# A rest group's expands in four row quadrants, rank rows copied as soon as their table is done, down's rank rows in one visit, and down's weight sums in two pieces

## The chip, the cores and the metric

The kernel runs on one core of a Trainium2 chip. The metric is the device time of one execution in microseconds (us). Everything is computed in float32. In the profile PE is TensorE (matmuls) and PEld its weight loads, DVE is VectorE, ACT is ScalarE, POOL is GpSimd, and SP is the queue that issues most DMA transfers.

## The reference

Eight sequences of 256 tokens with 1024 features pass four layers, each added to its input. Every layer picks low-rank adapters (rank 16) by an index per sequence:

```python
x = x + L0(x)   # x W^T + b, plus 2 * (x A) B            (A, B of 32 adapters)
x = x + L1(x)   # gate/up/down with 2752 hidden features, adapters on all three
x = x + L2(x)   # (x B^T) A^T only                        (64 adapters)
x = x + L3(x)   # (x B^T) A^T only                        (8 adapters)

# inside L1, SCALE = 0.5
gate = x @ W_gate.T + 0.5 * (x @ A_gate.T) @ B_gate.T
up   = x @ W_up.T   + 0.5 * (x @ A_up.T)   @ B_up.T
act  = silu(gate) * up
down = act @ W_down.T + 0.5 * (act @ A_down.T) @ B_down.T
```

The change touches L1 alone.

## The kernel before

**Blocks and banks.** The 2048 tokens are two blocks of 1024 (`blk`), and each block is two banks of 512 tokens (`n`), two sequences to a bank. Layer 0 is done for both blocks first, then gate/up, down, and the layers 2 and 3 of block 0, then those of block 1. Activations are kept transposed: features lie on the 128 partitions and tokens along the free dimension. A PSUM bank holds 128 x 512 values.

**Strassen-like products.** The large products are done as seven products of half-size blocks in place of eight, once outside and once more inside. `Quads.step` (L464) issues one outer product as seven inner blocks of matmuls (`block`, L473 to L482, all of them line L476), with adds on DVE and copies on ACT between them (`first` L504, `more` L509, `whole` L517). The last inner block of a product is put into `pending` and issued in the middle of the next product (`flush`). The order of the outer products is `ORDER = (1, 2, 3, 5, 6, 7, 4)`. The weights' sums that this needs are made on POOL: `inner_sums` and `outer` for gate/up, `Down.sum_weights` (L610) for down.

**Groups of gate/up.** The 2752 hidden features are cut into five groups of 512 (`job`, L998) and a rest of 192 (`rest`, L1099). In a block the rest comes first. A group gives four results: E (gate, bank 0), Z (up, bank 0), Y (up, bank 1) and X (gate, bank 1), which are done after the second, fifth, sixth and seventh outer product. In the code `table` 0 is gate and 1 is up. As a result is done, its `done(n, table, c)` is called.

**The rest group.** Its weights have 256 columns per table: gate has 192 features and then, in `wrem`, the up table's last 64; the up table has 128 features and then the adapters' shrink weights A_gate and A_up. So the second half of the up result holds the rank rows x A: 64 partitions of ranks, 16 for each sequence and table. When both tables of a bank are done, `done` in `rest` (L1117) puts this into the list `beside`:

- `spread(j)` for j = 0 and 1 (L1128): four ACT copies of 32 partitions of rank rows into the four quadrants of a PSUM bank, then a DVE product with a mask into `t`, the tile that the profile calls trep (L1135);
- `lora` (L1140): four matmuls of K = 32 with N = 512 from trep and the gathered B rows, all of them line L989 in `expand_gu`, into the three banks `lo` that the profile calls plr: gate's first 128 features from row quadrant 0, up's first 128 from row quadrant 0, and the last 64 of each, both from row quadrant 1, into the lower and upper half of the third bank;
- `gates` (sigmoids on ACT, L1149) and the adds and products on DVE (L1164 to L1169) that make the hidden rest `hr`, and then `hidden`, which puts the shrink for down (`shrink_hidden`, line L261) on PE.

In a full group `lora` (L1019 and before, tile pl) puts the four 128-feature chunks in the four quadrants, since the gathered table has 512 columns there: quadrant r holds chunk r. For the rest the host pads 192 features to 512, so that quadrants 2 and 3 hold zeros. trep holds the same rank rows in all four quadrants.

**What sets the order of the work.** Each outer product is a `Unit` with eight slots, `at(0)` to `at(7)`. In a slot the unit calls the loads and sums that are due there, and then takes items off the front of `beside` until their costs reach the unit's share (L1507 to L1513):

```python
spent = 0
while beside and spent < u.share:
    cost, f = beside.popleft()
    f()
    spent += cost
```

An item of cost 9 that does nothing therefore fills one slot. The framework's scheduler then places each engine's instructions in one fixed order, which needn't be the order of these calls, and adds the semaphore waits. Engines run their instructions in that order. SBUF tiles of 8 KB per partition come from one pool of 22 (`big`), PSUM banks for small work from a pool of four (`ps_l`), so an allocation can make an instruction wait for an earlier tile's last reader.

**Down.** `down_projection` (L1192) does the 2048 features of the first four groups by `Down`, seven outer products of two tables, and the remaining 704 features by `job` (L1286). For each of the seven products, `sum_weights` makes four sums of 128 x 1024 on POOL (L614 to L617). The rank rows of down, `td`, were added up over the groups; `rank_rows` (L1245) brings them under the rest's 64 features in `hr`: for each bank one matmul of M = 32 with a picking matrix (L1250, tile prr) into 32 partitions of one PSUM bank, and one DVE operation from there into `hr` (L1251).

Of the kernel before, what the change touches and what calls it, by code (L numbers as in the profile page):

```python
# [11 lines left out]
ALU = mybir.AluOpType  # L12

P = 128
# [11 lines left out]
NN = TB // 512  # L26
F = 2752
FC = 21
FR = F - FC * P
# [3 lines left out]
REST = len(GROUPS) - 1  # L33
# [21 lines left out]
def kernel(  # L55
# [48 lines left out]
    nc = tc.nc  # L104
# [14 lines left out]
    def big(name):  # L119
        return upool.tile([P, BIG], F32, tag="u", name=name)  # L120

    def bank(pool, name):
        return pool.tile([P, 512], F32, tag=pool.name, name=name)
# [5 lines left out]
    start = big("start")  # L129
# [29 lines left out]
    mask = const.tile([P, 512], F32, tag="mask", name="mask")  # L159
# [17 lines left out]
    for r in range(4):  # L177
        rows = slice(32 * r, 32 * r + 32)
# [5 lines left out]
    for r in range(4):  # L184
        rows = slice(32 * r, 32 * r + 32)
# [5 lines left out]
    for r in range(4):  # L191
        rows = slice(32 * r, 32 * r + 32)
        nc.vector.tensor_copy(off_23[rows], sel_v[rows, 2 + r % 2, :, r // 2])
    nc.vector.tensor_scalar(off_23, off_23, float(R), rank_f, op0=ALU.mult, op1=ALU.add)
    for r in (1, 3):
        rows = slice(32 * r, 32 * r + 32)
# [20 lines left out]
    pick = const.tile([P, 32], F32, tag="pick", name="pick")  # L217
# [20 lines left out]
    def gather_a(table, layer, blk, name, pool=apool, tag="a", width=NC * R):  # L238
        t = pool.tile([P, BB * width], F32, tag=tag, name=name)
        t = t[:, : BB * table.shape[1]].rearrange("p (b w) -> p b w", b=BB)  # L240
        for q in range(BB):
            b = blk * BB + q
            gather(t[:, q, :], table, off_a[:, layer, b : b + 1])
        return t
# [40 lines left out]
    def copy(dst, src, scale=1.0):  # L285
        nc.scalar.activation(dst, src, AF.Identity, scale=scale)  # L286
# [4 lines left out]
    beside = deque()  # L291
# [264 lines left out]
    class Down(Quads):  # L556
# [53 lines left out]
        def sum_weights(self, s):  # L610
            w = self.w[s]
            a11, a21, a12, a22 = w[0][:, 0], w[0][:, 1], w[2][:, 0], self.both[s][:, 1]
            s2, s4, s3 = w[1][:, 0], w[1][:, 1], w[2][:, 1]
            nc.gpsimd.tensor_sub(s3, a11, a21)  # L614
            nc.gpsimd.tensor_add(a21, a21, a22)
            nc.gpsimd.tensor_sub(s2, a21, a11)
            nc.gpsimd.tensor_sub(s4, a12, s2)  # L617

        def sum_tokens(self, s):
            h, both = self.h[s], self.both[s]  # L620
# [334 lines left out]
    def gate_up(blk):  # L955
        st = sts[blk]
# [16 lines left out]
        def shrink_hidden(g, *halves):  # L973

            a, chunks = st["ad", g]
            pss = []
            for n, h in halves:
                pss.append(bank(ps_l, f"pd_{blk}_{g}_{n}"))
                for r in range(len(h)):
                    shrink_into(pss[-1], r, a, chunks, r, n, h[r], True, True)  # L980
            for (n, h), ps in zip(halves, pss):
                rows, td = slice(0, 32 * len(h)), st["td"][n]
                if g == REST:
                    nc.vector.memset(td, 0.0)
                nc.vector.tensor_add(td[rows], td[rows], ps[rows])

        def expand_gu(table, n, g, r, ps, cols=slice(0, P), outs=slice(0, P)):
            rows = slice(32 * r, 32 * r + 32)
            nc.tensor.matmul(  # L989
                ps[outs],  # L990
                st["bgu", g][rows, table, n, cols],
                st["t"][rows, table, n, :],
                start=True,
                stop=True,
                skip_group_check=True,
            )
# [102 lines left out]
        def rest():  # L1099

            held = {}

            def raw(key, t):
                kh, table = int(key[1]) - 1, int(key[2]) - 1
                if table == 0:
                    nc.sync.dma_start(out=t, in_=wrem[kh, 0])
                    return
                nc.sync.dma_start(out=t[:, :512], in_=wrem[kh, 1, :, :512])

                w = t[:, 512:].rearrange("p (c m) -> p c m", m=P)  # L1110
                for j in range(2):
                    a = st["agu"][j].rearrange("p b (r c) -> p c (b r)", c=NC)
                    nc.scalar.copy(
                        w[:, :, j * BB * R : (j + 1) * BB * R], a[:, kh * HC : (kh + 1) * HC, :]
                    )

            def done(n, table, c):  # L1117
                c = c.rearrange("p q i j t -> p (q i) (j t)")
                held[n, table] = c
                if (n, 1 - table) not in held:  # L1120
                    return
                g, u = held[n, 0], held[n, 1]
                if "t" not in st:
                    st["t"] = big(f"trep_{blk}").rearrange("p (g n t) -> p g n t", g=2, n=NN)
                    st["hr"] = big(f"hr_{blk}").rearrange("p (c n t) -> p c n t", c=2, n=NN)
                t, hr = st["t"], st["hr"]
                lo = []

                def spread(j):

                    src = slice(64 * j + 32 * n, 64 * j + 32 * n + 32)
                    ps = bank(ps_l, f"pt_{blk}_{n}_{j}")
                    for r in range(4):
                        copy(ps[32 * r : 32 * r + 32], u[src, 1, :], 0.5)
                    nc.vector.tensor_mul(t[:, j, n, :], ps, mask)  # L1135

                for j in range(2):
                    beside.append((0.69, lambda j=j: spread(j)))

                def lora():  # L1140
                    for j in range(3):
                        lo.append(bank(ps_l, f"plr_{blk}_{n}_{j}"))
                    expand_gu(0, n, REST, 0, lo[0])
                    expand_gu(1, n, REST, 0, lo[1])
                    for j in range(2):
                        half = slice(FR * j, FR * j + FR)
                        expand_gu(j, n, REST, 1, lo[2], slice(0, FR), half)

                def gates():  # L1149
                    nc.scalar.activation(lo[0], g[:, 0], AF.Sigmoid)  # L1150
                    nc.scalar.activation(lo[2][:FR], g[:FR, 1], AF.Sigmoid)

                    copy(u[:FR, 1], g[FR:, 1])

                left = slice(0, FR)

                def hidden():
                    nc.vector.memset(hr[FR:, 1, n], 0.0)
                    held["hr", n] = [hr[:, 0, n], hr[:, 1, n]]
                    if ("hr", 1 - n) in held:  # L1160
                        shrink_hidden(REST, *((n, held["hr", n]) for n in range(NN)))

                def multiply(to, x, y):
                    beside.append((0.69, lambda: nc.vector.tensor_mul(to(), x(), y())))  # L1164

                beside.append((0, lora))
                beside.append((0.69, lambda: nc.vector.tensor_add(g[:, 0], g[:, 0], lo[0])))
                beside.append((0.69, lambda: nc.vector.tensor_add(u[:, 0], u[:, 0], lo[1])))
                beside.append((0.69, lambda: nc.vector.tensor_add(g[:, 1], g[:, 1], lo[2])))  # L1169
                beside.append((0, gates))  # L1170
                for a, b, c in ((g[:, 0], 0, slice(0, P)), (g[left, 1], 2, left)):
                    multiply(lambda b=b, c=c: lo[b][c], lambda a=a: a, lambda b=b, c=c: lo[b][c])
                multiply(lambda: hr[:, 0, n], lambda: u[:, 0], lambda: lo[0])
                multiply(lambda: hr[left, 1, n], lambda: u[left, 1], lambda: lo[2][left])
                beside.append((1.2, hidden))

            q = Quads(blk, f"1_{blk}_r", 1, raw, done, SHARE_REST)

            def shrink_tables():
                st["agu"] = [  # L1180
                    gather_a(t, 1, blk, f"agu_{blk}_{j}") for j, t in enumerate((ag, au))
                ]

            q.units[0].ahead.insert(0, (3, 0, shrink_tables))
            q.units[0].before(2, 0, lambda: tables(REST))
# [6 lines left out]
    def down_projection(blk):  # L1192
        st = sts[blk]
# [51 lines left out]
        def rank_rows():  # L1245

            ps = bank(ps_l, f"prr_{blk}")
            for n in range(NN):
                rows = slice(64 + 32 * n, 96 + 32 * n)
                nc.tensor.matmul(ps[rows], pick, st["td"][n], start=True, stop=True)  # L1250
                nc.vector.scalar_tensor_tensor(  # L1251
                    st["hr"][rows, 1, n], ps[rows], 0.5, mask[rows], op0=ALU.mult, op1=ALU.mult
                )

        def load_w(o, g):
# [219 lines left out]
        for o in range(HC):  # L1475
            u = Unit(f"2_{blk}_{o}", lambda at, o=o: job(o, at), 1.2)
# [170 lines left out]
```

## Time and profile before

| what | value |
| --- | --- |
| median of 3 runs | 1804.67 us (1803.13 to 1806.73) |
| profiled execution, own time | 1805.19 us |
| its span, first to last instruction | 1803.4 us |
| mean granted TensorE clock | 0.998 |
| PE busy | 1790.4 us (99%) |
| DVE busy | 1051.5 us (58%) |
| POOL busy | 984.1 us (55%) |
| ACT busy | 298.6 us (17%) |
| DMA, mean over the span | 224 GB/s |

The profile is of one execution. A matmul of float32 stands in it as two records, and so does each weight load. Lengths of PE's records overlap, since matmuls are pipelined: the time that a piece of PE's work takes is read from its start to the start of the next piece. In the rows of the timeline, what stands in brackets is the idle time of the engine before the row and what ended it. "issue" means that the engine waited for nothing that the profile shows.

The chain of work that ended last is PE for 93% of the span. Its largest lines are the gate/up products (pa L476 26%, pc L476 13%, pb L476 6%), down's products (pa_d L476 11%, pc_d L476 5%, pb_d L476 3%) and L375 (pa 10%, pc 5%, pb 2%). The rest's products (pa_r L476) are 2% and the full groups' expands (pl L989) 2%.

### The profile page before, as it was taken

The numbers are of one execution on the slowest core, as the hardware profiler recorded it, in microseconds if no ns is written. First come the engines' busy times: TensorE is split into PE (matmuls) and PEld (weight loads), VectorE is DVE, ScalarE is ACT, GpSimd is POOL, SyncE is SP. The second block draws the span as 40 slices with busy tenths as digits, with TensorE's granted clock in tenths as the row PEclk, the third lists the DMA queues.
The fourth block names the chain that finished last, engine by engine and source line by source line (L and its number), as shares of the span: only waits on it lengthen the run. The fifth ranks groups of instructions, "written<-read, shape, count | busy, mean of one in ns | idle before, by whom it ended". The sixth has DMA issues, their size and how long they took to land.

```text
span 1803.4 us, 20672 instructions
## 1 busy us (share of the span) xinstructions
PE 1790.4 (99%) x7664; PEld 1312.2 (73%) x7664; DVE 1051.5 (58%) x1675; ACT 298.6 (17%) x536; POOL 984.1 (55%) x742
## 2 busy tenths in 40 slices
PE   9999999999999999999999999999999999999998
PEld 4444477888787878788854678787888887888743
DVE  5584255666666666748842464757575758554623
ACT  0121023020202121224210031121212121221000
POOL 6202579685868686344530567676767564443301
PEclk9999999999999999999999999999999999999999
DMA  6476895867676755778831865575848475745302
GB/s 233 172 281 250 273 396 184 304 225 287 215 294 208 298 187 217 260 272 311 316 135 67 307 264 192 176 292 171 296 165 290 166 256 184 255 165 180 110 0 94
DMA packets 119094, 403.38 MB, mean 224 GB/s; under 512 B 11858, under 2 KB 42706, under 8 KB 109522
## 3 DMA queue, kind: packets, MB, share of 16 engines
q1 hardware_dynamic: 108752, 382.24, 58.4%
q0 software_dynamic: 6080, 12.99, 2.3%
q10 hardware_dynamic: 4162, 6.82, 1.2%
q8 instruction: 62, 1.02, 0.2%
q14 instruction: 38, 0.31, 0.0%
HBM read 317.59 MB, written 84.41 MB: 223 GB/s over the span
## 4 chain that ended last, share of the span: by engine, by line
PE 93%; DVE 3%; issue 2%; DMA 1%; POOL 0%; ACT 0%; DVEq 0%; POOLq 0%; ACTq 0%; SPq 0%
PE pa L476 26%; PE pc L476 13%; PE pa_d L476 11%; PE pa L375 10%; PE pb L476 6%; PE pc_d L476 5%; PE pc L375 5%; PE pb_d L476 3%; PE pb L375 2%; PE pl L989 2%; PE pa_r L476 2%; PE pp L875 2%; PE pd L261 1%; PE pc_r L476 1%; DMA w_B<-in_wgu_dram 1%
## 5 line engine op out<-in xcount | busy, mean ns | idle before, releaser
L476 PE MATMUL pa<-tk,sw 128*128 128x256 f32 x1120 | 268.9, 383 | 1.7 <-DVE c_X L507 1.7
L476 PE MATMUL pc<-tk,sw 128*128 128x256 f32 x1120 | 264.9, 379 | 0.3 <-POOL sw L447 0.3
L476 PEld LDWEIGHTS pa<-tk,sw 128*128 128x128 f32 x1120 | 209.0, 190 | 59.9 <-issue 10.6
L476 PEld LDWEIGHTS pc<-tk,sw 128*128 128x128 f32 x1120 | 212.5, 190 | 31.2 <-issue 1.8
L476 PE MATMUL pa<-tk,w_B 128*128 128x256 f32 x960 | 227.8, 380 | 0.0
L476 PEld LDWEIGHTS pa<-tk,w_B 128*128 128x128 f32 x960 | 181.6, 190 | 32.5 <-issue 6.5
L446 POOL TENSOR_TENSOR sw<-w_B 128x512 f32<-128x512 f32 x60 | 76.5, 1275 | 170.8 <-PE pa L476 151.3
L614 POOL TENSOR_TENSOR dx_d<-dw_d 128x1024 f32<-128x1024 f32 x14 | 33.0, 2356 | 164.7 <-PE pa L476 44.3
L476 PE MATMUL pb<-tk,w_B 128*128 128x256 f32 x480 | 113.4, 379 | 0.0
L476 PE MATMUL pa_d<-dh_d,dw_d 128*128 128x256 f32 x448 | 102.2, 379 | 0.0
L476 PE MATMUL pc_d<-dh_d,dw_d 128*128 128x256 f32 x448 | 101.7, 379 | 0.0
L476 PEld LDWEIGHTS pb<-tk,w_B 128*128 128x128 f32 x480 | 91.2, 190 | 12.4
L507 DVE TENSOR_TENSOR c_X<-c_X,pa 128x512 f32<-128x512 f32 x90 | 61.5, 683 | 64.9 <-PE pa L476 64.9
L437 POOL TENSOR_TENSOR w_B<-w_B,w_B 128x1024 f32<-128x1024 f32 x40 | 93.4, 2356 | 2.4 <-PE pa L476 2.4
L476 PEld LDWEIGHTS pa_d<-dh_d,dw_d 128*128 128x128 f32 x448 | 85.0, 190 | 12.4 <-issue 0.8
L476 PEld LDWEIGHTS pc_d<-dh_d,dw_d 128*128 128x128 f32 x448 | 85.0, 190 | 12.4 <-issue 0.8
L448 POOL TENSOR_TENSOR sw<-w_B 128x512 f32<-128x512 f32 x60 | 87.8, 1463 | 0.0
L449 POOL TENSOR_TENSOR sw<-w_B,sw 128x512 f32<-128x512 f32 x60 | 80.6, 1343 | 3.9
L447 POOL TENSOR_TENSOR sw<-sw,w_B 128x512 f32<-128x512 f32 x60 | 76.9, 1282 | 0.0
L286 ACT ACTIVATE c_X<-pa 128x512 f32<-128x512 f32 x30 | 17.7, 591 | 341.1 <-PE pa L476 341.1
L231 POOL DMA_INDIRECT ad<-in_ad_dram,off_a x48 | 46.1, 961 | 31.3 <-PE pd L261 20.9
L375 PE MATMUL pa<-ht,wd 128*128 128x512 f32 x128 | 60.2, 600 | 0.0
(380 smaller groups left out, 3118.1 us busy)
## 6 DMA issues: line engine op xcount, KB each, us to landing
tk<-toks SPq DMA_DIRECT2D x140, 896.0 KB, 6.6
w_B<-in_wgu_dram SPq DMA_DIRECT2D x40, 1024.0 KB, 5.0
tk_r<-toks SPq DMA_DIRECT2D x28, 896.0 KB, 11.0
hk<-c_Z SPq DMA_DIRECT2D x32, 512.0 KB, 4.1
dh_d<-hk SPq DMA_DIRECT2D x14, 1024.0 KB, 8.4
hk<-c_Y SPq DMA_DIRECT2D x24, 512.0 KB, 4.1
x1d<-x SPq DMA_DIRECT2D x8, 1024.0 KB, 6.4
wo<-in_wd_dram SPq DMA_DIRECT2D x8, 1024.0 KB, 7.0
```

The lines of the kernel that those rows point to most:

```text
L231: nc.gpsimd.indirect_dma_start(out=t, out_offset=None, in_=table, in_offset=bass.IndirectOffsetOnAxis(ap=off, axis=0),)
L375: nc.tensor.matmul(ps, v[j], m[j], start=start and k == 0, stop=k == len(moving) - 1, skip_group_check=True,)
L437: f(self.raw[out][:, c], self.raw[a][:, c], self.raw[b][:, c])
L446: nc.gpsimd.tensor_add(s1, m21, m22)
L447: nc.gpsimd.tensor_sub(s2, s1, m11)
L448: nc.gpsimd.tensor_sub(s3, m11, m21)
L449: nc.gpsimd.tensor_sub(s4, m12, s2)
L476: nc.tensor.matmul(ps[:, q, :], w(j, q, kk), tok(j, kk), start=start and q == 0 and kk == 0, stop=kk == self.deep - 1, skip_group_check=True,)
L507: nc.vector.tensor_add(view(out, r, k), view(old, r, k), ps)
L614: nc.gpsimd.tensor_sub(s3, a11, a21)
L875: nc.tensor.matmul(pss[j, n], st["w", o][:, i, j // HC], x[c][n], start=i == 0, stop=i == NC - 1,)
L989: nc.tensor.matmul(ps[outs], st["bgu", g][rows, table, n, cols], st["t"][rows, table, n, :], start=True, stop=True, skip_group_check=True,)
```

## The change

There are four edits.

1. The rest's four expands take the row quadrants 0, 2, 1 and 3 in place of 0, 0, 1 and 1. For this the host repeats the padded 256 columns of B twice in place of padding to 512.
2. The rest's rank rows are copied as soon as the up table of a bank is done. For bank 0, where the gate table is done before, six empty items of cost 9 follow the copies, so that `lora` is called six slots later. For bank 1, where the up table is done first, the copies are put into `beside` one outer product earlier than before. The tiles trep and hr are allocated when the first result is done.
3. `rank_rows` issues both matmuls and then both DVE operations, in place of one after the other.
4. `sum_weights` makes each of the four sums in two pieces of 128 x 512. In the built program the two pieces of one sum stand next to each other on POOL.

```diff
@@ sum_weights
-            nc.gpsimd.tensor_sub(s3, a11, a21)
-            nc.gpsimd.tensor_add(a21, a21, a22)
-            nc.gpsimd.tensor_sub(s2, a21, a11)
-            nc.gpsimd.tensor_sub(s4, a12, s2)
+            for k in range(2):
+                c = slice(k * 512, k * 512 + 512)
+                nc.gpsimd.tensor_sub(s3[:, c], a11[:, c], a21[:, c])
+                nc.gpsimd.tensor_add(a21[:, c], a21[:, c], a22[:, c])
+                nc.gpsimd.tensor_sub(s2[:, c], a21[:, c], a11[:, c])
+                nc.gpsimd.tensor_sub(s4[:, c], a12[:, c], s2[:, c])
@@ rest: done
                 held[n, table] = c
-                if (n, 1 - table) not in held:
-                    return
-                g, u = held[n, 0], held[n, 1]
                 if "t" not in st:
                     st["t"] = big(f"trep_{blk}").rearrange("p (g n t) -> p g n t", g=2, n=NN)
                     st["hr"] = big(f"hr_{blk}").rearrange("p (c n t) -> p c n t", c=2, n=NN)
                 t, hr = st["t"], st["hr"]
                 lo = []
+                ranks, both = c, (n, 1 - table) in held
...
                     for r in range(4):
-                        copy(ps[32 * r : 32 * r + 32], u[src, 1, :], 0.5)
+                        copy(ps[32 * r : 32 * r + 32], ranks[src, 1, :], 0.5)
                     nc.vector.tensor_mul(t[:, j, n, :], ps, mask)
 
-                for j in range(2):
-                    beside.append((0.69, lambda j=j: spread(j)))
+                if table == 1:
+                    for j in range(2):
+                        beside.append((0.69, lambda j=j: spread(j)))
+                    if both:
+                        for _ in range(6):
+                            beside.append((9, lambda: None))
+                if not both:
+                    return
+                g, u = held[n, 0], held[n, 1]
 
                 def lora():
                     for j in range(3):
                         lo.append(bank(ps_l, f"plr_{blk}_{n}_{j}"))
-                    expand_gu(0, n, REST, 0, lo[0])
-                    expand_gu(1, n, REST, 0, lo[1])
+                    for j in range(2):
+                        expand_gu(j, n, REST, 2 * j, lo[j])
                     for j in range(2):
                         half = slice(FR * j, FR * j + FR)
-                        expand_gu(j, n, REST, 1, lo[2], slice(0, FR), half)
+                        expand_gu(j, n, REST, 2 * j + 1, lo[2], slice(0, FR), half)
@@ rank_rows
             ps = bank(ps_l, f"prr_{blk}")
+            rows = [slice(64 + 32 * n, 96 + 32 * n) for n in range(NN)]
             for n in range(NN):
-                rows = slice(64 + 32 * n, 96 + 32 * n)
-                nc.tensor.matmul(ps[rows], pick, st["td"][n], start=True, stop=True)
+                nc.tensor.matmul(
+                    ps[rows[n]], pick, st["td"][n], start=True, stop=True, skip_group_check=True
+                )
+            for n, r in enumerate(rows):
                 nc.vector.scalar_tensor_tensor(
-                    st["hr"][rows, 1, n], ps[rows], 0.5, mask[rows], op0=ALU.mult, op1=ALU.mult
+                    st["hr"][r, 1, n], ps[r], 0.5, mask[r], op0=ALU.mult, op1=ALU.mult
                 )
@@ on the host: the rest's gathered B rows
-        t = np.pad(t, ((0, 0), (0, 0), (0, 0), (0, 4 * P - (f1 - f0))))
+        t = np.pad(t, ((0, 0), (0, 0), (0, 0), (0, -(f1 - f0) % (2 * P))))
+        t = np.tile(t, 4 * P // t.shape[-1])
```

## The prediction

> **What bounds the kernel now.** I read the page's busy line first, then PE's waits, then PE's timeline at the places that the change touches. A row of the timeline is: start, length, engine, line, operation, out<-in, shape, number of records.
>
> ```profile
> PE 1790.4 (99%) x7664; PEld 1312.2 (73%) x7664; DVE 1051.5 (58%) x1675; ACT 298.6 (17%) x536; POOL 984.1 (55%) x742
> ```
>
> PE is busy 99% of 1803.4 us. All its listed waits come to about 5.6 us, so a few us can be won only by giving PE less to stream or by removing those waits:
>
> ```profile
> PE plr L989 <- DVE trep L1135: 1.9, 3, 0.8
> PE pa L476 <- DVE c_X L507: 1.7, 2, 0.8
> PE pc L476 <- POOL sw L447: 0.3, 1, 0.3
> ```
>
> No down weight (dw_d, dx_d) is among them. PE's timeline around the rest group of block 0 (each f32 matmul has two records):
>
> ```profile
> 264.17 1.03 PE L476 MATMUL pc_r<-tk_r,sw_r 128*128 128x256 f32 x4
> 265.80 2.98 PE L989 MATMUL plr<-trep,bgu 32*128 32x512 f32 x8 [0.60 <-DVE trep L1135]
> 268.71 1.13 PE L476 MATMUL pa_r<-tk_r,w_r_T 128*128 128x256 f32 x4
> ...
> 278.10 1.12 PE L989 MATMUL plr<-trep,bgu 32*128 32x512 f32 x2
> 279.15 1.99 PE L476 MATMUL pa<-tk,sw 128*128 128x256 f32 x8
> 281.08 2.12 PE L989 MATMUL plr<-trep,bgu 32*128 32x512 f32 x6
> 283.13 1.99 PE L476 MATMUL pc<-tk,sw 128*128 128x256 f32 x8
> ...
> 307.82 1.14 PE L989 MATMUL pl<-trep,bgu 32*128 32x512 f32 x8
> 308.89 1.99 PE L476 MATMUL pa<-tk,sw 128*128 128x256 f32 x8
> ```
>
> Compare start to next start. Four full-width K=32 expands in four quadrants (pl) take 1.07 us. The four of the rest (plr) take 2.91 us, or 1.05 + 2.05 = 3.10 us. The loads say how plr splits:
>
> ```profile
> 266.76 0.18 PEld L989 LDWEIGHTS plr<-trep,bgu 32*128 32x128 f32 x1 [0.19 <-issue]
> 267.70 0.19 PEld L989 LDWEIGHTS plr<-trep,bgu 32*64 32x64 f32 x4 [0.76 <-issue]
> ```
>
> The two 128-wide ones follow each other in quadrant 0. The two 64-wide halves run side by side, 267.70 to 268.71, 1.01 us, but start only when the 128-wide ones are through (second pass about 267.19 plus 0.43), though they stand in another quadrant. So a change of tile width is a barrier here.
>
> In block 1 the same group is followed by a loss that no wait shows (columns: stretch and its length, busy us of PE, PEld, DVE, ACT, POOL, then the granted clock):
>
> ```profile
> 1048.80:1052.20 3.40, 2.65 (x8) 0.85 (x8) 2.94 (x7) 1.10 (x2) 0.00 (x0) 1.00 1.00 417
> 1052.20:1055.60 3.40, 3.40 (x9) 2.41 (x8) 1.68 (x4) 1.22 (x2) 1.64 (x2) 0.50 0.31 125
> ```
>
> Half clock for 3.4 us of PE-bound work is 1.7 us lost.
>
> **The change, part by part.**
>
> *Quadrants.* The pair in quadrants 0 and 2 now overlaps: 1.05 us, the price of one alone at 278.10. The halves keep 1.01 us: 2.06 per group. Saved: block 0, n=0: 2.91 - 2.06 = 0.85; n=1: 3.10 - 2.06 = 1.04. Block 1, n=0: 1049.55 to 1052.66 is 3.11, less 0.23 at half clock = 2.88, saved 0.82; n=1: 1.05 + 2.05, saved 1.04. Sum 3.75 us. The host's doubled table changes no instruction.
>
> Here a rule speaks against the change: the halves now sit in row quadrants 1 and 3 and write one bank, lo[2]. The Trainium skill, TensorEngine Tiling, section Gotcha 1: PSUM Pressure, says that different row tiles cannot access the same PSUM bank at once. No row of this trace has two row quadrants on one bank; the nearest row is the old halves (one row quadrant, one bank, two column halves, side by side in 1.01). By the rule each group is 0.86 longer (two passes of 0.43), 3.4 us in all. I take the row: the halves land on different partitions (0-63, 64-127).
>
> *Rank rows earlier.* Sixteen ACT copies per block (0.6 us each) and four mask products stay the same in number. In the order as built, n=0's four expands stand behind both matmuls of Y's last block. Block 0: PE came free at 265.03 and waited 0.76; now it arrives at 265.90, the pair starts at 265.95 and 266.40 (second mask product ends at 266.34), so about 0.4 is left: saved 0.35. Block 1: the group moves by one matmul (0.43), the first mask product still ends at 1049.5, the second 0.6 later, and the pair needs both: lost 0.1. Block 1, n=1: the copies of Y start right after Y instead of five us later; the wait (1063.13 against 1062.45) goes: saved 0.68.
>
> New queueing, block 0: ACT's first copy of Y (0.6) and the 1.28 us table load now stand before the sigmoid. DVE's product behind it holds the next evacuation (L507), which PE's fourth rest block needs: about 0.6 late. Then the first pc of group 0 is pulled forward and waits for DVE's pc_r evacuation, about 0.45, where it already waited 0.48 at 275.34. The halves of n=1 now reuse the bank that n=0's product into hr frees, and that product stands behind X's last add: 0.3. Net loss 0.87. Sum of waits: 0.35 - 0.1 + 0.68 - 0.87 = 0.06. These are estimates from the rows' durations; bounds -2 and +2.
>
> *The half clock.* In block 1 the stretch without full-array matmuls is 1048.55 to 1052.66, 4.1 us; it becomes 1048.98 to about 1052.05, 3.1 us, shorter than the 3.4 us of the granted-clock window. The Trainium skill (TensorE: Matmul & The Clock Gate, Part 1) throttles after a whole idle window of about 3.4 us, free-running. By that rule the stretch, shown busy 2.65 of 3.40, should not have tripped it, and the change could not cure it: 0. By the row, low load is enough, and the cure is 1.7. I take the row, 1.7.
>
> *Rank rows of down, one visit.* PE now:
>
> ```profile
> 870.98 1.04 PE L1250 MATMUL prr<-td,pick 128*32 128x512 f32 x2
> 871.96 0.70 PE L476 MATMUL pa_d<-dh_d,dw_d 128*128 128x256 f32 x2
> ...
> 872.93 0.59 PE L476 MATMUL pa_d<-dh_d,dw_d 128*128 128x256 f32 x2
> 873.45 1.05 PE L1250 MATMUL prr<-td,pick 128*32 128x512 f32 x2
> ```
>
> A visit is 0.98 plus 0.09 ahead of it (872.93 to 873.45 for a matmul of 0.43) = 1.07. Two column strips side by side take one visit (pd: four such matmuls, two strips in two rounds, 288.51 to 290.35, 0.92 a round). Two blocks: 2 x 1.07 = 2.1 us. If they don't overlap, 0.2.
>
> *Down sums in two steps.* 56 POOL operations on 128x1024 become 112 on 128x512. Now a step's four cost 2.356 + 2.428 + 2.415 + 2.454 = 9.65; eight pieces at 1.27 (the wo sums, same shape, L767 to L770) are 10.16: 0.5 more, 7 us over 14 steps. Both pieces of one operation stand next to each other, so the last sum isn't earlier, and no transfer is issued differently: SP's order is unchanged. Its cover is PE's lead: the tightest sum (L615 of block 0's fifth step) starts at 826.77, ends at 829.13, and PE's first use is at 838.95, 9.8 us later. Cost 0; uncovered, 7 us.
>
> **Sum.** 3.75 + 0.06 + 1.7 + 2.1 = 7.6 us. The profiled execution has 1805.19 us with a span of 1803.4, so 1.8 lies outside: 1803.4 - 7.6 + 1.8 = 1797.6. It lies 0.5 above the median of 1804.67, and the three runs differ by 3.6, about two half-clock windows; I say 1797.5.
>
> **The rivals.**
> - *One bank, two row quadrants, in turn*: +3.4, 1801.0. For it the rule above; against it that the partitions differ.
> - *The half clock stays*: +1.7, 1799.3. For it: the window runs freely, so another 3.4 us can catch the group.
> - *All four overlap across widths, as pl does*: a group of 1.07, another 0.99 x 4 = 4.0 saved, 1793.5. Against it the late load at 267.70.
> - *Slower: POOL becomes the bound in down.* A down product takes PE seven blocks of 3.45 = 24.2 us; eight pieces pass that at 3.0 us a piece. At 3.2 us, 14 x 8 x 0.18 = 20 us: 1818. For it: POOL's 128x1024 rows reach 2.80 beside 2.36, so it is disturbed at times; against: that is a fifth, and a piece needs more than twice its 1.27.
> - *No gain (the change doesn't do what it says)*: strips and pairs don't overlap and new waits take 2 more: about 1804.
>
> **How the numbers follow.** What is told from no change is about 0.2%, 3.6 us: below 1801.1 is faster, above 1808.3 slower. Chances: likeliest 0.55 (own range 1795.5 to 1799); half clock stays 0.16; bank in turn 0.14; all four at once 0.06; no gain 0.05; slower 0.04. Faster is the first two, the fourth and half of the third, 0.83; slower 0.04; the rest, 0.13, is same. The range leaves out the last two and half of the fourth: 1794 to 1802.
>
> **What would show it.** plr groups of 8 records taking about 2.06 us start to start (2.9: bank in turn; 1.07: all at once); no wait of PE on trep in n=1; one visit of prr per block of about 1.07 with 4 records; the granted clock 1.00 through both rest groups; POOL about 7 us busier with PE not waiting for dw_d. The forecast is wrong if PE shows a new wait behind ACT's table load longer than 0.6 us, or a half-clock stretch that was not there.

## The result, and the profile after

| | before | after |
| --- | --- | --- |
| median, us | 1806.18 (1803.13 to 1806.73, 6 executions) | 1796.01 (1793.30 to 1796.50, 6 executions) |
| ratio | | 0.9943, 95% interval 0.9930 to 0.9956 |
| span of the profiled execution, us | 1803.4 | 1794.7 |
| DVE busy, us | 1051.5 | 1042.4 |
| POOL busy, us | 984.1 | 992.9 |

The time fell by 0.57%. The forecast was 1797.5 us, 1794 to 1802, with 0.83 for faster. The total is right, but two of its terms are not: the half clock, which was counted, was not cured in the profiled execution, and the down sums, counted at nothing, brought 1.94 us.

Where the 8.7 us of span went can be read by comparing the start of the same matmul in both traces. What the difference grows by at one place is the saving of that place:

| place | saved, us | forecast, us |
| --- | --- | --- |
| first 10 us (no edit there) | 0.28 | 0 |
| rest group of block 0 | 1.41 | 1.37 |
| end of block 0's last gate/up group | 0.96 | 0 |
| rank rows of down, block 0 | 1.17 | 1.07 |
| rest group of block 1 | 2.55 | 2.44 + 1.7 (half clock) |
| end of block 1's last gate/up group | 0.98 | 0 |
| rank rows of down, block 1 | 1.16 | 1.07 |
| end of the execution, and rounding | 0.2 | 0 |

(1.37 is 0.35 + 0.85 + 1.04 - 0.87 of the prediction, and 2.44 is 0.82 + 1.04 - 0.1 + 0.68. Both profiled executions hold one window at half clock in block 1.)

The busy line of the page after:

```profile
PE 1784.2 (99%) x7664; PEld 1311.2 (73%) x7664; DVE 1042.4 (58%) x1675; ACT 299.0 (17%) x536; POOL 992.9 (55%) x798
```

PE is the bound as before. POOL has 56 more instructions and 8.8 us more work, yet DVE has 9.1 us less, with the same 1675 instructions. That is the first sign of what the prediction missed. PE's waits after (waiting tile, releaser: us in total, times, longest):

```profile
PE pa_r L476 <- DVE c_r_X L507: 0.5, 1, 0.5
PE plr L992 <- DVE trep L1136: 0.4, 1, 0.4
PE pl L992 <- ACT dh_d L286: 0.4, 2, 0.2
PE pc L476 <- POOL sw L448: 0.4, 1, 0.4
```

The 1.9 us for trep became 0.4, and the two waits of 0.84 us of pa for DVE's c_X (L507) are gone. The 0.5 is new, and was forecast (0.6, behind ACT's table load). The two of 0.2 for ACT's dh_d are new as well; the kernel with edit 4 alone has them too. PE's timeline after, at the places of the edits:

```profile
264.91 1.13 PE L476 MATMUL pa_r<-tk_r,w_r_T 128*128 128x256 f32 x4
265.98 2.26 PE L992 MATMUL plr<-trep,bgu 32*128 32x512 f32 x8
268.17 1.13 PE L476 MATMUL pa_r<-tk_r,sw_r 128*128 128x256 f32 x4
...
271.55 1.13 PE L476 MATMUL pa_r<-tk_r,sw_r 128*128 128x256 f32 x4 [0.52 <-DVE c_r_X L507]
...
273.48 0.67 PE L476 MATMUL pc<-tk,sw 128*128 128x256 f32 x2 [0.37 <-POOL sw L448]
...
277.53 2.25 PE L992 MATMUL plr<-trep,bgu 32*128 32x512 f32 x8
279.72 1.99 PE L476 MATMUL pa<-tk,sw 128*128 128x256 f32 x8
...
717.09 1.99 PE L476 MATMUL pa<-tk,sw 128*128 128x256 f32 x8
...
868.33 1.05 PE L1259 MATMUL prr<-td,pick 128*32 128x512 f32 x4
869.32 0.70 PE L476 MATMUL pa_d<-dh_d,dw_d 128*128 128x256 f32 x2
```

Both groups of block 0 take 2.19 us from start to start (268.17 - 265.98; 279.72 - 277.53). At 717.09 pa starts without a wait. The rank rows are one visit of 0.99 us with four records. The loads of the first group, on PEld:

```profile
265.97 0.43 PEld L992 LDWEIGHTS plr<-trep,bgu 32*128 32x128 f32 x4 [0.33 <-issue]
267.16 0.19 PEld L992 LDWEIGHTS plr<-trep,bgu 32*64 32x64 f32 x4 [0.76 <-issue]
```

The pair's four loads now stand within 0.43 us, and the halves still come after them, together. In block 1 (busy us of PE, PEld, DVE, ACT and POOL in each stretch, then the granted clock):

```profile
1044.80:1048.20 3.40, 2.98 (x11) 0.89 (x9) 3.37 (x8) 1.34 (x4) 1.06 (x1) 1.00 0.99 412
1048.20:1051.60 3.40, 3.40 (x9) 2.52 (x8) 2.67 (x5) 3.28 (x6) 3.40 (x4) 0.50 0.35 140
```

The half clock still follows the rest group, though PE's wait and the group together are 0.7 us shorter than before: 1045.15 to 1048.50 in place of 1048.55 to 1052.66.

### The profile page after: what moved, and what is told of

It reads as the page before. It is cut to its first block, busy times and chain, and to the rows that moved or that the text cites. A ratio compares the mean times of both kernels' runs of the same rounds, so it can differ in the third digit from the quotient of the medians.

```text
span 1794.7 us, 20739 instructions
## 1 busy us (share of the span) xinstructions
PE 1784.2 (99%) x7664; PEld 1311.2 (73%) x7664; DVE 1042.4 (58%) x1675; ACT 299.0 (17%) x536; POOL 992.9 (55%) x798
## 4 chain that ended last, share of the span: by engine, by line
PE 96%; DVE 3%; DMA 1%; issue 0%; POOL 0%; ACT 0%; DVEq 0%; ACTq 0%; SPq 0%; POOLq 0%
PE pa L476 26%; PE pc L476 13%; PE pa_d L476 11%; PE pa L375 10%; PE pb L476 6%; PE pc_d L476 5%; PE pc L375 5%; PE pb_d L476 3%; PE pb L375 2%; PE pl L992 2%; PE pa_r L476 2%; PE pp L878 2%; PE pd L261 1%; PE pc_r L476 1%; PE p L261 1%; PE p L276 1%
## 5 line engine op out<-in xcount | busy, mean ns | idle before, releaser
L617 POOL TENSOR_TENSOR dx_d<-dw_d 128x512 f32<-128x512 f32 x28 | 37.3, 1353 | 159.3 <-PE pa L476 42.0
L507 DVE TENSOR_TENSOR c_X<-c_X,pa 128x512 f32<-128x512 f32 x90 | 61.5, 683 | 64.6 <-PE pa L476 64.6
```

What stands on the lines that cost most here:

```text
L507: nc.vector.tensor_add(view(out, r, k), view(old, r, k), ps)
L617: nc.gpsimd.tensor_sub(s3[:, c], a11[:, c], a21[:, c])
```

## The experiments

Ratios are to executions of the kernel before on the same chip beside them. A time in brackets is the median of those.

### Each edit alone

Each kernel is the one before with one of the four edits, as in the diff above (`...` marks what is left out here).

**Quadrants (edit 1).**

```diff
-                    expand_gu(0, n, REST, 0, lo[0])
-                    expand_gu(1, n, REST, 0, lo[1])
+                    for j in range(2):
+                        expand_gu(j, n, REST, 2 * j, lo[j])
...
-                        expand_gu(j, n, REST, 1, lo[2], slice(0, FR), half)
+                        expand_gu(j, n, REST, 2 * j + 1, lo[2], slice(0, FR), half)
...
```

> The kernel before with edit 1 alone: the rest's four expands take row quadrants 0, 2, 1, 3. By the prediction's step, the pair of 128-wide expands overlaps and the halves stay side by side: a group of 8 records takes 2.06 us from start to start in place of 2.9 to 3.1, and the time falls by 3.75 us, less what PE then waits longer for the second mask product (0.2 or so per group). By the rival of one bank in turn, a group takes 2.9 us and the time falls by 0.3 us at most. If the half clock behind block 1's group goes with the shorter group, another 1.7 us.

Measured: 1804.29 us (1805.22), ratio 0.9993 (0.9984 to 1.0001). That is neither 3.75 nor the 0.3 of the rival: the two 128-wide expands rarely meet. PE's timeline of bank 1's group in block 0, in this kernel:

```profile
276.94 1.12 PE L989 MATMUL plr<-trep,bgu 32*128 32x512 f32 x2
277.99 1.99 PE L476 MATMUL pa<-tk,sw 128*128 128x256 f32 x8
279.92 2.12 PE L989 MATMUL plr<-trep,bgu 32*128 32x512 f32 x6
```

As before the change, the scheduler puts an inner block of eight records between the first expand and the other three, so the pair cannot run side by side, whatever its quadrants. In bank 0 the second of the pair waits 0.30 us for its mask product; that group takes 2.65 us against 2.91. So edit 1 alone shortens one group of block 0, by 0.26 us; in block 1 a stretch at half clock covers the end of bank 0's group, and bank 1's is split again. In the changed kernel it is edit 2, which has the rank rows ready, that brings all four together.

**Rank rows early (edit 2).**

```diff
...
-                for j in range(2):
-                    beside.append((0.69, lambda j=j: spread(j)))
+                if table == 1:
+                    for j in range(2):
+                        beside.append((0.69, lambda j=j: spread(j)))
+                    if both:
+                        for _ in range(6):
+                            beside.append((9, lambda: None))
...
```

> The kernel before with edit 2 alone: rank rows copied once their table is done, six empty items ahead of bank 0's expands, quadrants as before. Prediction: a sum of waits of 0.06 us saved (0.35 - 0.1 + 0.68 - 0.87), so no change, within 1 us. Rival: the queueing behind ACT's table load is larger than worked out, and the time rises by 1 to 2 us. Of the half clock in block 1: by the reading of the prediction (low load over a window trips it) it should stay here, since the group keeps its 3.1 us; if it depends on where the free-running window stands, it may be anywhere or absent.

Measured: 1803.91 us (1805.22), ratio 0.9992 (0.9985 to 0.9998). All four groups now stand in one piece of 2.91 us, and the idle time ahead of them falls: 0.76 to 0.09 (bank 0, block 0), 1.00 to 0.58 and 0.68 to 0.09 (block 1). Each of the two groups that is no longer split takes 0.19 less. New waits take part of it back: 0.3 and 0.4 us for DVE's c_r_X. In the trace 0.13 us is left in block 0 and 1.4 in block 1, where 0.06 in all was forecast; the medians differ by 1.3. The half clock at the rest group is absent from its profile and one stands at 1516.88 us instead, so it does not depend on that group's length alone (the group keeps its 2.91 us here).

**Rank rows of down in one visit (edit 3).**

```diff
             for n in range(NN):
-                nc.tensor.matmul(ps[rows], pick, st["td"][n], start=True, stop=True)
+                nc.tensor.matmul(
+                    ps[rows[n]], pick, st["td"][n], start=True, stop=True, skip_group_check=True
+                )
+            for n, r in enumerate(rows):
                 nc.vector.scalar_tensor_tensor(
-                    st["hr"][rows, 1, n], ps[rows], 0.5, mask[rows], op0=ALU.mult, op1=ALU.mult
+                    st["hr"][r, 1, n], ps[r], 0.5, mask[r], op0=ALU.mult, op1=ALU.mult
...
```

> The kernel before with edit 3 alone: both matmuls of down's rank rows in one visit. Prediction: 2 x 1.07 = 2.1 us less. If the two column strips did not run side by side, 0.2 us less. The two waits of 0.84 us before pa stand as before in either case.

Measured: 1800.40 us (1805.22), ratio 0.9968 (0.9956 to 0.9980), 4.8 us. In the trace the edit's two places save 1.17 us each, a little more than the 1.07 forecast, since the matmul behind a visit also comes 0.1 us sooner. Most of the rest of the 4.8 seems to be half clock: the profiled execution has no such window before its last 8 us, and the mean granted clock of its executions is 0.9980 against 0.9969 of the kernel before, which is 2 us of 1800. Whether the edit itself lowers the odds of half clock is not shown. With six executions a median can be off by about one window at half clock (1.7 us), and the trace is the better witness for edits of this size.

**Down sums in two pieces (edit 4).**

```diff
-            nc.gpsimd.tensor_sub(s3, a11, a21)
...
+            for k in range(2):
+                c = slice(k * 512, k * 512 + 512)
+                nc.gpsimd.tensor_sub(s3[:, c], a11[:, c], a21[:, c])
...
```

> The kernel before with edit 4 alone: down's weight sums in two pieces. Prediction: 0, POOL 7 us busier. New theory, from the two traces: at the end of a block's last gate/up group, DVE's adds with both inputs in SBUF (c_Z, c_X) are held until the 128x1024 operation on POOL ends, which makes the next evacuation late and PE wait 0.84 us before pa at two places; shorter pieces hold them less, so both waits go and the time falls by 2 x 1.07 = 2.1 us. Against it: if those waits went because of the other edits, 0 here and both waits stand.

Measured: 1802.06 us (1805.22), ratio 0.9980 (0.9971 to 0.9989). In the trace the two places save 0.96 and 0.97 us, and both waits of PE for DVE's c_X are gone; with each of the other three edits alone they stand unchanged at 1.7 us in all. The gain is edit 4's.

### Why shorter POOL operations help PE

DVE in the kernel before, at the end of block 0's last gate/up group:

```profile
708.04 2.22 DVE L519 TENSOR_TENSOR c_Z<-c_Z,c_X 128x512 f32<-128x512 f32 x1
710.18 0.67 DVE L507 TENSOR_TENSOR c_X<-c_X,pa 128x512 f32<-128x512 f32 x1
...
713.22 2.29 DVE L519 TENSOR_TENSOR c_Z<-c_Z,c_X 128x512 f32<-128x512 f32 x1
...
719.01 0.68 DVE L507 TENSOR_TENSOR c_X<-c_X,pa 128x512 f32<-128x512 f32 x1
```

POOL in the kernel before, at the same time:

```profile
707.36 2.35 POOL L614 TENSOR_TENSOR dx_d<-dw_d 128x1024 f32<-128x1024 f32 x1 [11.19 <-PE pa L476]
709.79 2.68 POOL L615 TENSOR_TENSOR dw_d<-dw_d,db_d 128x1024 f32<-128x1024 f32 x1
712.61 2.35 POOL L616 TENSOR_TENSOR dw_d<-dw_d 128x1024 f32<-128x1024 f32 x1
```

PE at the same time:

```profile
717.02 1.89 PE L476 MATMUL pb<-tk,w_T 128*128 128x256 f32 x8
719.75 1.99 PE L476 MATMUL pa<-tk,sw 128*128 128x256 f32 x8 [0.84 <-DVE c_X L507]
```

DVE's add L519 has both inputs in SBUF and takes 0.69 us elsewhere. Here it ends at 710.26, 0.55 after POOL's L614 (709.71), and at 715.51, 0.55 after L616 (714.96): it gets through only when POOL's operation is about done. L507 at 710.18, with one input in PSUM, takes 0.67 in the middle of POOL's L615. Of the two delays, 1.53 and 1.60 us, the first costs nothing, since DVE waits for PE before 712.50 anyway. Behind the second DVE's queue has no gap until L507 at 719.01, and PE waits for that. DVE after:

```profile
706.35 1.14 DVE L519 TENSOR_TENSOR c_Z<-c_Z,c_X 128x512 f32<-128x512 f32 x1
...
711.53 1.32 DVE L519 TENSOR_TENSOR c_Z<-c_Z,c_X 128x512 f32<-128x512 f32 x1
...
716.36 0.68 DVE L507 TENSOR_TENSOR c_X<-c_X,pa 128x512 f32<-128x512 f32 x1
```

Two pieces let DVE in between them: the delays are 0.45 and 0.63. The second is 0.97 shorter than before, and that is what this place saves. The Trainium skill (SBUF — State Buffer, Who interferes with whom) states the mechanism: that a DVE instruction with two SBUF inputs contends with a GpSimd instruction that reads SBUF, not with one that only writes it, and that the shared ports are an exclusive lock, held for the whole instruction. The last experiment of this part puts the word "reads" to the test:

```diff
+            if s == 0:
+                for x in (s3, a21, s2, s4):
+                    for _ in range(2):
+                        nc.gpsimd.memset(x, 0.0)
+                return
             nc.gpsimd.tensor_sub(s3, a11, a21)
```

> The kernel before, with the sums of the first of down's seven products left out: in their place POOL writes zeros into the same four tiles, each twice, 128x1024. Theory of the shared reads: DVE's adds with two inputs in SBUF are held only by a POOL operation that reads SBUF; a memset reads nothing, so the adds (c_Z, c_X, L519) beside it take 0.69 us, DVE L507 is on time, and PE's two waits of 0.84 us go: 2.1 us less. Theory of any POOL operation (or of POOL's writes): the adds end with the memsets, as long as those last, and stay over 1 us wherever a memset starts first.

Measured: 1802.53 us (1805.73), ratio 0.9983 (0.9976 to 0.9989). DVE and then POOL in this kernel:

```profile
708.16 0.69 DVE L519 TENSOR_TENSOR c_Z<-c_Z,c_X 128x512 f32<-128x512 f32 x1
...
713.34 0.69 DVE L519 TENSOR_TENSOR c_Z<-c_Z,c_X 128x512 f32<-128x512 f32 x1
```

```profile
707.46 1.96 POOL L617 MEMSET dx_d<- 128x1024 f32 x2 [4.45 <-PE pa L476]
712.64 3.64 POOL L617 MEMSET dw_d<- 128x1024 f32 x4 [3.22 <-PE pa L476]
```

Both adds begin in the middle of memsets (two take 1.96 us, four 3.64) and take 0.69 us, and PE's two waits are gone; each place saves 1.1 us. POOL is at work beside both adds and writes the same tiles, but reads nothing. So it is what POOL reads that holds DVE, not that it is busy or that it writes.

### What halves the clock

Within an execution, all stretches at half clock start on one grid of 3.413 us (in the trace after, 1048.22 and the tail's 1788.91 are 217.0 periods apart); the grid's offset differs between executions. For each window of these grids I summed, over PE's matmuls in it, the streaming time (as at full clock) weighted with the share of the array that the tile covers: a matmul of K = 32 rows and M = 128 columns counts a quarter. I call the sum the array use. Over 14 traces, leaving out the first 60 us and the tail, all 15 windows with less than 1.26 us of such use are followed by one at half clock, none with 1.29 or more is, and of three at 1.26 and 1.27 two are. With the rows alone as weight the two kinds part less well: 11 windows without half clock behind them lie below the highest one with it. Two kernels test it; the first adds four matmuls of K = 32, the second the same with 128 in place of 32:

```diff
                 def lora():
                     for j in range(3):
                         lo.append(bank(ps_l, f"plr_{blk}_{n}_{j}"))
+                    for _ in range(4 if n == 0 else 0):
+                        nc.tensor.matmul(
+                            lo[2],
+                            st["bgu", REST][:32, 0, n, :],
+                            st["t"][:32, 0, n, :],
+                            start=True,
+                            stop=True,
+                            skip_group_check=True,
+                        )
```

> The changed kernel with four more matmuls of K = 32, M = 128, N = 512 ahead of bank 0's expands of the rest in each block; the expands overwrite what they leave. They use one row quadrant one after the other: 4 x 0.86 = 3.44 us more a block, 6.9 us in all. What is tested is what halves the clock. New theory: a window of 3.41 us in which the array is filled to less than a third, by the tiles' area times their streaming time, is followed by one at half clock. Then each block has one or two windows at half clock behind this place, 1.7 us each: 1796 + 6.9 + 1.7 to 5 us, and the granted clock shows a half window behind the rest group of both blocks. If only a window without work halves the clock, the same time as with K = 128, and no half clock here, since PE is busy throughout.

> As the one with K = 32, but the four added matmuls have K = 128 (all 128 partitions of the same tiles): the same streaming time, 6.9 us in all, at four times the area. By the theory of the area no window at half clock behind the rest groups, or one by chance as after the change: 1796 + 6.9 = 1803 us or up to 1.7 less, and 1.7 to 5 us faster than with K = 32. By the theory of the window without work, the same time as with K = 32.

Measured: K = 32 1829.00 us, ratio 1.0000 (0.9992 to 1.0009); K = 128 1822.95 us, ratio 0.9969 (0.9957 to 0.9981). These two and the next two kernels ran on a chip on which the first 60 us take some 23 us longer in all four traces, and the kernel before is as much slower too (1828.76), so only ratios and places behind the start are compared. At K = 32 the windows of the grid at the rest group of block 0:

```profile
290.97:294.38 3.41, 3.41 (x12) 1.47 (x10) 1.17 (x4) 2.06 (x3) 0.00 (x0) 1.00 1.03 426
294.38:297.79 3.41, 3.41 (x8) 0.94 (x7) 2.46 (x4) 2.17 (x4) 2.85 (x3) 0.50 0.72 293
297.79:301.20 3.41, 3.41 (x10) 2.69 (x9) 1.46 (x4) 3.25 (x7) 3.41 (x3) 0.50 0.03 11
```

At K = 128, the same place:

```profile
289.60:293.00 3.40, 3.40 (x11) 1.62 (x9) 2.27 (x6) 0.97 (x2) 0.00 (x0) 1.00 1.02 423
293.00:296.40 3.40, 3.40 (x14) 1.29 (x13) 1.70 (x3) 2.52 (x4) 1.64 (x2) 1.00 1.03 422
```

In the window 290.97 to 294.38 PE is busy 3.41 of 3.41 us, but that is only 1.06 us of array use, and two windows at half clock follow; so they do in block 1 (from 1079.44). At K = 128 there is none outside the start and the tail. Four windows are 4 x 1.7 = 6.8 us; the medians differ by 6.05. A window without work, the Trainium skill's condition (TensorE: Matmul & The Clock Gate, Part 1), is not needed. The two kernels differ in rows alone; that columns count as well rests on the 14 traces.

### The bank rule and the width barrier

**Both halves from row quadrant 1**, in the changed kernel:

```diff
-                        expand_gu(j, n, REST, 2 * j + 1, lo[2], slice(0, FR), half)
+                        expand_gu(j, n, REST, 1, lo[2], slice(0, FR), half)
```

> The changed kernel with both 64-wide halves from row quadrant 1, as before the change, in place of quadrants 1 and 3; nothing else is changed. If two row quadrants on one bank cost nothing, as the prediction took it, groups and time are the same (1796 us, groups 2.06 to 2.19). If they cost something that the trace after hides (0.13 of the 2.19), a group is 0.1 shorter here.

Measured: 1820.36 us (1828.76), ratio 0.9951 (0.9936 to 0.9966). The groups take 2.19, 2.19, 2.65 and 2.06 us from start to start. The changed kernel, run again, has 2.19, 2.19, 2.65 and 2.06. So two row quadrants that write one bank, on different partitions (0 to 63 and 64 to 127), cost nothing here.

**All four expands 128 wide**, in the changed kernel, with a fourth bank and one more add:

```diff
-                    for j in range(3):
+                    for j in range(4):
                         lo.append(bank(ps_l, f"plr_{blk}_{n}_{j}"))
-                    for j in range(2):
-                        expand_gu(j, n, REST, 2 * j, lo[j])
-                    for j in range(2):
-                        half = slice(FR * j, FR * j + FR)
-                        expand_gu(j, n, REST, 2 * j + 1, lo[2], slice(0, FR), half)
+                    for i in range(2):
+                        for j in range(2):
+                            expand_gu(j, n, REST, 2 * j + i, lo[2 * i + j])
...
-                beside.append((0.69, lambda: nc.vector.tensor_add(g[:, 1], g[:, 1], lo[2])))
+                for x, h in ((2, slice(0, FR)), (3, slice(FR, P))):
+                    beside.append((0.69, lambda x=x, h=h: nc.vector.tensor_add(g[h, 1], g[h, 1], lo[x][h])))
...
+            t[1, ..., 3 * P + FR :] = t[1, ..., P : P + FR]
+            t[1, ..., 3 * P : 3 * P + FR] = 0
```

> The changed kernel with the rest's four expands all 128 wide, in four quadrants and four banks: the host puts up's last 64 columns into columns 64 to 127 of its second chunk, and one add of 128 partitions becomes two of 64. If a change of tile width is the barrier, as the prediction has it, a group takes 1.07 us in place of 2.06 to 2.19 and the time falls by four times 1.0 to 1.1, to about 1792 us. If something else separates the pairs (their loads, their banks), a group stays at about 2 us and the time at 1796. A loss is possible too: a fourth bank of the pool of four is held during the adds, and whatever small work comes next waits for it.

Measured: 1816.22 us (1828.76), ratio 0.9937 (0.9923 to 0.9951). The groups take 1.20, 1.34, 1.66 and 1.34 us, 3.55 less than in the changed kernel: the tile width is the barrier. (The halves' shared bank is not: the pair that they waited for writes two others, and the halves themselves ran side by side.) But the time is at most some 1.3 us below the changed kernel's (ratio 0.9944, below), which is within the intervals. PE's timeline:

```profile
288.80 1.27 PE L992 MATMUL plr<-trep,bgu 32*128 32x512 f32 x8
...
294.44 1.13 PE L476 MATMUL pa_r<-tk_r,sw_r 128*128 128x256 f32 x4 [1.58 <-DVE c_r_X L507]
```

PE comes to this block a microsecond earlier and finds DVE a further add behind: it waits 1.58 us in place of 0.52, and 0.92 at the same place of block 1, where there was no such wait.

**The extra add moved** behind ACT's copy. The diff is against the last kernel, whose edit on the host is also taken back, so that the third bank's upper half adds zeros:

```diff
-                for x, h in ((2, slice(0, FR)), (3, slice(FR, P))):
-                    beside.append((0.69, lambda x=x, h=h: nc.vector.tensor_add(g[h, 1], g[h, 1], lo[x][h])))
+                beside.append((0.69, lambda: nc.vector.tensor_add(g[:, 1], g[:, 1], lo[2])))
...
                 multiply(lambda: hr[:, 0, n], lambda: u[:, 0], lambda: lo[0])
+                beside.append((0.69, lambda: nc.vector.tensor_add(u[left, 1], u[left, 1], lo[3][left])))
```

> The changed kernel with the rest's four expands 128 wide in four quadrants and four banks, as in four_at_once, but with the extra add moved: the third add stays at 128 partitions (its upper half adds zeros), ACT's copy of up's last 64 stays behind the sigmoids, and up's expand is added after that copy. DVE then has one add of 0.7 us less ahead of the evacuation (L507) for which four_at_once made PE wait 1.58 and 0.92 us. If DVE's queue makes that wait, each falls by about 0.7 and the time is 1.3 us less than four_at_once, some 3 us less than the changed kernel (ratio to the kernel before about 0.9925). If ACT's sigmoid behind the table load makes it, the waits stay and the ratio is that of four_at_once, 0.9937.

> The changed kernel once more, beside the others, to compare with: 0.9943 of the kernel before. Windows at half clock, 1.7 us each, come or not with the position of a free-running grid: the mean clock of its executions should differ in steps of one or two thousandths, and the times with it.

Measured: 1793.74 us, ratio 0.9936 (0.9923 to 0.9950); the changed kernel beside it 1794.58 us, 0.9944 (0.9930 to 0.9958). DVE's queue did make the wait (1.58 became 0.74 and 0.92 went), but bank 1's group now takes 2.61 us. Its loads, on PEld:

```profile
275.55 0.67 PEld L992 LDWEIGHTS plr<-trep,bgu 32*128 32x128 f32 x4 [0.33 <-issue]
276.52 0.29 PEld L992 LDWEIGHTS plr<-trep,bgu 32*128 32x128 f32 x2 [0.30 <-DVE hr L1171]
277.11 0.29 PEld L992 LDWEIGHTS plr<-trep,bgu 32*128 32x128 f32 x2 [0.30 <-DVE hr L1171]
```

By the profile, the third and fourth expand wait for DVE's products into hr, which are the last to read bank 0's part of the pool of four PSUM banks.

**Four wide in bank 0 only**, as the changed kernel in bank 1:

```diff
-                    for j in range(3):
+                    for j in range(4 - n):
...
+                        if n == 0:
+                            expand_gu(j, n, REST, 2 * j + 1, lo[2 + j])
+                            continue
...
```

> As four_later_add for bank 0, and as the changed kernel for bank 1, which then needs three PSUM banks, not four. If the fourth bank is what bank 1's group waited for in four_later_add (2.61 us), that group falls to the 2.06 to 2.19 of the changed kernel, bank 0's stays at 1.20 and 1.66 with a wait of about 0.7 behind it: 2 x 0.45 us less than four_later_add, a ratio of about 0.993 to the kernel before, against 0.9944 for the changed kernel. If the group stays at 2.6, the wait is not for the bank.

Measured: 1793.73 us (1804.81), ratio 0.9940 (0.9926 to 0.9953). Bank 1's groups are 2.43 us, between the two expectations, and their halves still wait for a product into hr; so the fourth bank was part of the wait at most, and the rest stays open. PE waits 1.7 us for L507 again. None of the three kernels can be told apart from the changed one. What bank 0's groups save is given back at DVE's queue and in bank 1's groups.

## Why the prediction was right, and where not

**Quadrants and rank rows, 3.75 + 0.06.** Measured 1.41 + 2.55 = 3.96. The sum is right, and so are most of its details: no wait on trep for bank 1, a new wait of 0.52 behind the table load (0.6), one of 0.37 at the pulled pc (0.45; the profile puts it down to POOL's sw, where the working had DVE). What failed is how it was shared out. The prediction took a pair that overlaps as edit 1's work, 1.04 for each of bank 1's groups, and the earlier rank rows as 0.06. By the medians edit 1 alone wins 0.9 us (not clear of the noise) and edit 2 alone 1.3, so some 1.7 us (an estimate, 3.96 less these two) come only with both, since the order as built splits bank 1's groups. The 2.06 of a group was met once; block 0's two are 2.19, and block 1's bank 0 takes 2.65 in the changed kernel run again, since there the second mask product is 0.6 late, which the prediction had booked as part of a wait.

**The half clock, 1.7.** This step failed as stated. "Low load" was the right side of the row against the rule, as the K = 32 kernel shows, but it was read as an event tied to this group, which a stretch shorter than 3.4 us would end. It is a matter of chance with a price: a window with less than about 1.27 us of array use is followed by half clock, the grid lies anywhere, and after the change many positions still hold one (1044.80 to 1048.20 has 0.96). The profiled execution after has its window; the one run again has none. Over executions the change does lower the odds: the mean granted clock is 0.9968 before (65 executions) and 0.9979 after (11), about 1.9 us of 1800. Moving the grid through all positions of a trace, with the stretches at half clock counted at full clock and 1.15 or 1.25 us as the bound, gives 1.7 to 2.2 low windows an execution before and 0.3 to 0.7 in the changed kernel's two traces (an estimate). So a term of about 2 us belongs in the sum of medians, but not in the comparison of two traces, and the rival "half clock stays" was true of the trace.

**Rank rows in one visit, 2.1.** Measured 1.17 + 1.16, with four records in 0.99. The working left out that a visit also holds back the matmul behind it, by 0.1.

**Down sums, 0.** This is the step that failed. POOL's cost (8.8 us against 7) and its cover (PE waits for no dw_d) were right, but the working asked only who waits for the sums. It did not ask who works beside them: DVE was held by them at two places, and PE waited for DVE. The wait stood among the lines shown of before, as 1.7 us of PE for DVE's c_X, and its cause was not followed further; the add of 2.29 us a few rows ahead of it would have told. 0.96 + 0.98 us were missing.

**Rivals.** One bank in turn fell with the halves in one quadrant. All four across widths fell too: the widths are a barrier, and four equal ones take 1.20 to 1.66. POOL as the bound did not come near: PE has no wait for down's weights.

The errors point in opposite directions, and that the total fell within its range is in part luck. Between the profiled executions, -1.7 and +1.94 nearly cancel; the rest of the way from 7.6 to 8.7 us is 0.28 ahead of any edit and some tenths elsewhere. On the medians, where part of the half clock does go, the gain is 10 to 11 us (1806.18 to 1796.01; 1805.73 to 1794.58), and 7.6 was too little by the down sums and a little more. The forecast time came closer than the gain, since it started from a median of 1804.67, which six executions put at 1806.18. (The chances as listed add up to 0.84 for faster, not 0.83.)

## What to carry to other kernels

Before a wait is costed, follow it one step further: a DVE row with two SBUF inputs that takes several times its usual length and ends shortly after a POOL operation may be held by that operation, and cutting POOL's work into shorter pieces can pay even when nobody waits for its result. Edits that need each other should be costed together: here matmuls in different quadrants overlapped only where the scheduler left them next to each other and all had one tile width. Where the clock halves now and then, count array use over a window, not busy time, and put it into the forecast as odds times price.

## What the runs showed of the hardware that was not expected

- PE busy for a whole window can still have its clock halved: 3.41 us of matmuls of K = 32, one after the other, were enough (1.06 us of array use). The bound lies between 1.26 and 1.29 us of 3.41, about 0.37.
- A DVE add with two SBUF inputs beside a POOL operation of 2.35 us took 2.22 and 2.29 us in place of 0.69; beside memsets 0.69.
- Two row quadrants with 64-wide tiles on different partitions of one bank cost nothing (groups of 2.19, 2.19, 2.65 and 2.06 us with either one or two quadrants); a change of tile width between 128 and 64 costs 0.7 to 1.0 us a group, against four tiles of 128.
